# First attention of a fused transformer kernel: the masked queries are made by GpSimd from one unmasked tile, instead of by ScalarE

## The chip, the core and the metric

The kernel runs on one core of one Trainium2 chip. The time is that of the device, in microseconds (us): of several runs the median is taken. Engines are named as the profile names them: PE is TensorE (PEld its loading of weights), DVE is VectorE, ACT is ScalarE, POOL is GpSimd and SP is SyncE, which issues most of the DMAs.

## What is computed

Two layers, each an attention followed by a mixture-of-experts feed-forward. x has 64 sequences of 128 tokens of 128 features, in float32. In short:

```
x = x + attention0(layernorm(x), keys and values from a side input and from a context)
x = x + experts0(layernorm(x))         # 8 experts, the best 2 for each token
x = x + attention1(layernorm(x), keys and values from the context)
x = x + experts1(layernorm(x))         # 8 experts, the best 2 for each token

def attention0(x1, x2, memory):        # 16 heads of 8 features
    q = (x1 @ Wq + bq) split into heads
    k = concatenate(x2 @ Wk + bk, memory) split into heads     # 128 + 120 keys
    v = concatenate(x2 @ Wv + bv, memory) split into heads
    return (softmax(q @ k.T * 8 ** -0.5) @ v) @ Wp + bp
```

The change concerns q of attention0 alone.

## The kernel before

**Heads and slots.** A head has only 8 features, so four heads share a block of 32 partitions. To get the scores of one head out of a matmul over 32 partitions, the queries of the other three are set to zero. Hence every group's queries are stored four times, once for each of NS = 4 slots s, with only the rows of that slot's heads kept: the tile `q4` of 128 partitions x (4 sequences, 4 slots, 128 queries). The mask is a column of `hmask`, a one or a zero for each partition. The rows left empty take the running maximum of the scores later (`shift`, L455 to L464: VectorE adds it into `q4`, L462), so that the second set of matmuls gives scores from which the maximum is already subtracted.

**Groups and iterations.** The 64 sequences are 16 groups g of 4. `attention` (L232) runs one iteration per sequence, and in one iteration several sequences are at different stages. In iteration `it` of the first attention the order of the work is written out by hand (all engines take their instructions in the order in which the program gives them):

- `rounds(0, 1)`: for sequence it, `max_bank` (matmul L394, then the maximum over the keys by VectorE, L414); for sequence it-2, `score_bank` (matmul L430, then the exponential by ScalarE, L438). Each round takes four PSUM banks, two of each kind.
- `out4` (L511), `shift` (transposes L459, then L462), `out5` (L516), statistics of layernorm (`bn_stats`, L109), one call of the router of the experts (`Router.call`, L641).
- `values` (L475, 64 matmuls in four accumulating chains), `out1` (ScalarE's copy L484).
- `prep(it, 0)`, a second call of the router, `rounds(2, 3)`.
- `out3` (L504, L506), `out2` (L491, L495, L497), `prep(it, 1)`.

PSUM is one pool of eight banks (`banks`, tag `bank`); every tile of PSUM is one of them and goes back when its last reader is done.

**Preparing a group's queries.** `prep` (L339) spreads the preparation of the next group over the four iterations of the current one. In the last of them, `prep_x` (L279) transposes the normalized tokens (TensorE, L176) and ScalarE copies them to `xnT` (L177), a tile with a single buffer. In the first iteration of the next group, `prep_q(g, 0)` (L289) runs the matmul with Wq (L292) into one bank and two of ScalarE's activations (L301), and `prep_q(g, 1)`, behind `rounds(2, 3)`, the other two. Each reads the 128x512 bank, adds the bias, applies the mask as its scale and writes one slot of `q4`. So the queries of group g are made in the four iterations ahead of those that read them, except for group 1, where both halves run at the start of iteration 3. Group 0 goes another way (`prep_batch`, L320, four activations of 128x128 for each sequence). `q4` has three buffers. The second attention uses `prep_q` too, and has made an unmasked copy as well (`qfs`, L295).

**GpSimd's queue.** In the first attention GpSimd makes the layernorm (`put_together`, L138 to L146, and the normalization L167), once for the attention itself and once for the router; it adds the output bias to x (L526), computes three products of the router for every second group (L761, L764, L769, between which VectorE reduces, L763, L768, L771) and issues the scatters of the routed tokens (indirect DMA L807, each behind a small copy L806). VectorE takes the router's small steps (`best`, L705, with L718 to L735; `dispatch`, L818, with L836 to L861) in `Router.call`, in between the maxima of the rounds.

**Later stages.** After the first attention, the tiles of the experts (`tile_stage`, L1050), then the second attention with the second set of experts inside it.

Of the kernel before, what the change touches and what calls it, by code (L numbers as in the profile page):

```python
# [8 lines left out]
F32 = mybir.dt.float32  # L9
I32 = mybir.dt.int32  # L10
AF = mybir.ActivationFunctionType
ALU = mybir.AluOpType
# [6 lines left out]
GB = 4  # L19
NG = B // GB  # L20
S = 128
D = 128
# [22 lines left out]
def transformer_kernel(ctx, tc, a, out):  # L45
    nc = tc.nc
# [25 lines left out]
    def load_const(name, shape, src):  # L72
        t = const.tile(shape, F32, name=f"c_{name}", tag=f"c_{name}")
        nc.sync.dma_start(t, src)
        return t

    def load_row(name, n):
        return load_const(name, [128, n], a[name].partition_broadcast(128))

    def attention_weights(p, names=("wq", "wk", "wv", "wo", "bq", "bk", "bv", "bo")):  # L80
        columns = {"bq": NS, "bk": NV, "bqf": 1}
        return {
            n: load_row(p + n, D) if n in ("bv", "bo")
            else load_const(p + n, [D, columns.get(n, D)], a[p + n])
            for n in names
        }

    l0 = attention_weights("a0_", ("wk", "bk"))
# [96 lines left out]
    for s in range(2):  # L185
        k = keep.tile([128, NV, GB, KF + KC], F32, name=f"k2_{s}", tag=f"k2_{s}")
        K2.append(k)
        v = keep.tile([KF, GB, H // 2, 2, 32], F32, name=f"v_{s}", tag=f"v_{s}")
# [43 lines left out]
    def attention(layer, w, norm, first, aside):  # L232
# [5 lines left out]
        with ExitStack() as es:  # L238
            work = es.enter_context(tc.tile_pool(name=f"work{layer}", bufs=2))
# [4 lines left out]
            if first:  # L244
                for s in range(2):
                    v = work.tile([128, GB, H // 2, 2, 32], F32, name="vc", tag="vc")
# [3 lines left out]
            qfs, k4s = {}, {}  # L250
            src, q4s, xnTs, ps_, pavs, pts, ots, normed = {}, {}, {}, {}, {}, {}, {}, {}
# [24 lines left out]
            def mtile():  # L276
                return banks.tile([128, 512], F32, name="bank", tag="bank")
# [11 lines left out]
            def prep_q(g, v):  # L289
                if v == 0:  # L290
                    pqs[g] = mtile()
                    nc.tensor.matmul(pqs[g], lhsT=w["wq"], rhs=xnTs[g], start=True, stop=True)  # L292
                pq = pqs[g]
                if v == 0 and not first:
                    nc.scalar.activation(  # L295
                        qfs[g], pq.rearrange("p (b q) -> p b q", b=GB), AF.Identity,
                        bias=w["bqf"],
                    )
                for i in range(2):
                    s = 2 * v + i  # L300
                    nc.scalar.activation(  # L301
                        q4s[g][:, :, s, :], pq.rearrange("p (b q) -> p b q", b=GB),
                        AF.Identity, bias=w["bq"][:, s : s + 1], scale=hmask[:, s : s + 1],
                    )
# [34 lines left out]
            def prep(it, half):  # L339

                g, j = it // GB + 1, it % GB
                if not first:
                    if g == 1:
                        if (j, half) == (0, 0):
                            prep_k(1)
                            prep_v(1)
                        elif (j, half) == (0, 1):
                            prep_x(1)
                        elif j == 1:
                            prep_q(1, half)  # L350
                            if half:
                                prep_heads(1)
                    elif g < NG:
                        pieces = (
                            (), (lambda: prep_k(g),),
                            (lambda: (prep_heads(g), prep_v(g)), lambda: prep_x(g)),
                            (lambda: prep_q(g, 0), lambda: prep_q(g, 1)),
                        )[j]
                        if half < len(pieces):
                            pieces[half]()  # L360
                    return
# [9 lines left out]
                if (it, half) == (3, 0):  # L371
                    prep_q(1, 0)
                    prep_q(1, 1)
# [923 lines left out]
    aside0 = Aside0()  # L1297
    steps = attention(0, l0, norms[0], True, aside0)
    next(steps)
    l0.update(attention_weights("a0_", ("wq", "bq")))  # L1300
    hmask = load_const("hmask", [128, NS], a["hmask"])
    next(steps)
    l0.update(attention_weights("a0_", ("wv", "bv")))
# [178 lines left out]
def _laid_out(inp):  # L1482

    import numpy as np

    A = {k: np.asarray(v) for k, v in inp.items()}

    def moved(w):
        w = w.reshape(-1, NV, 4, 2 * HD)[:, ::-1]
        return w.transpose(0, 2, 1, 3).reshape(-1, D)  # L1490

    heads = np.arange(D).reshape(4, NV, 2, HD)
    hm, km, sm = (np.zeros((D, n), np.float32) for n in (NS, NV, NV))
    for v in range(NV):
        km[heads[:, 1 - v].ravel(), v] = 1.0
        sm[np.arange(4) * 32 + 16 * v, v] = 1.0
        for i in range(2):
            hm[heads[:, 1 - v, i].ravel(), 2 * v + i] = 1.0

    o = {"x": A["x"]}  # L1500
    o["fsideT"] = A["fside_BxSxS_0"].transpose(2, 0, 1)
    c = A["ctx_1024"]
    o["ctxT"] = c.transpose(2, 0, 1)
    k = moved(c.reshape(B * KC, D)).reshape(B, KC, 1, D)
    o["ctx_k"] = np.where(km.T > 0, k, sm.T).transpose(3, 2, 0, 1)
    v = np.zeros((B, KC, H // 2, 2, 32), np.float32)
    for i in range(2):
        v[:, :, :, i, 16 * i : 16 * i + HD] = c.reshape(B, KC, H // 2, 2, HD)[:, :, :, i]
        v[:, :, :, i, 16 * i + HD] = 1.0
    o["ctx_v"] = v.reshape(B, KC, H * 32).transpose(1, 0, 2)  # L1510
    o["hmask"], o["kmask"], o["smask"] = hm, km, sm
    for p, l, names, tr in (
        ("a0_", "L0_xattn_", ("Wq", "bq", "Wk", "bk", "Wv", "bv", "Wp", "bp"), False),
        ("a1_", "L1_xattn_", ("W_q", "b_q", "W_k", "b_k", "W_v", "b_v", "W_o", "b_o"), True),
    ):
        wq, bq, wk, bk, wv, bv, wo, bo = (A[l + n] for n in names)
        if tr:
            wq, wk, wv, wo = wq.T, wk.T, wv.T, wo.T
        o[p + "wq"], o[p + "wk"] = moved(wq), moved(wk)
        o[p + "bq"] = np.where(hm > 0, moved(bq).T, np.float32(0.0))  # L1520
        if tr:
            o[p + "bqf"] = moved(bq).T
        o[p + "bk"] = np.where(km > 0, moved(bk).T, sm)
        o[p + "wv"], o[p + "bv"] = wv, bv
        o[p + "wo"], o[p + "bo"] = wo, bo
    o["wqkvT"] = A["L0_ffn_wqkv"].T

    w1 = np.zeros((E, D, 2, NF * 128), np.float32)
    w1[..., :F] = A["L0_ffn_w1"].reshape(E, 2, F, D).transpose(0, 3, 1, 2)
    w2 = np.zeros((E, NF * 128, D), np.float32)  # L1530
    w2[:, :F] = A["L0_ffn_w2"].transpose(0, 2, 1)
    w12 = np.concatenate(
        [w1.reshape(E, D, 2, NF, 128).transpose(0, 1, 3, 2, 4).reshape(E, D, NF, 256),
         w2.reshape(E, NF, 128, D).transpose(0, 2, 1, 3)], axis=3,
    )
    o["w12"] = w12.reshape(E, D, NF * 384)
    o["upper"] = np.triu(np.ones((128, 128), np.float32), 1)
    o["ones"] = np.ones((128, 128), np.float32)
    o["steps256"] = np.arange(CAP // TT, dtype=np.float32) * TT

    t = np.zeros((4, 32, 4, 2, 64), np.float32)
    for e in range(E):
        t[:, e, e // 2, e % 2, :] = 1.0
    o["select"] = t.reshape(128, 4, 128)
    o["tiles"] = np.arange(NA, dtype=np.float32).reshape(1, -1)
    o["row_number"] = np.arange(1, 129, dtype=np.float32).reshape(-1, 1)
    o["first_row"] = np.arange(E, dtype=np.float32) * CAP
    o["wgT"] = A["L1_ffn_Wg"].T
    o["bg"] = A["L1_ffn_bg"]
    o["lw1T"] = A["L1_ffn_W1"].transpose(2, 0, 1).reshape(D, E * R)  # L1550
    o["lw2T"] = A["L1_ffn_W2"].transpose(0, 2, 1).reshape(E * R, D)
    return {k: np.ascontiguousarray(v) for k, v in o.items()}
# [18 lines left out]
```

## Time and profile before

| what | value |
|---|---|
| time, median of 3 runs | 1477.64 us (1471.13 to 1481.87) |
| the profiled execution, time | 1476.76 us |
| its span, first to last instruction | 1474.9 us |
| granted TensorE clock, mean | 0.987 |
| instructions | 42033 |
| ACT, all of the four slots (L301), both attentions | 90.1 us busy in 124 instructions |
| POOL, all | 647.0 us busy in 1195 instructions |
| first attention, period of one group | 37.0 to 37.7 us, 41.3 us for the one at 499.7 us |

The times are those of one execution, taken by the hardware profiler. A row of the groups gives a line, an engine and an operation, out<-in by tile names with their shapes, xcount, then busy us and mean ns of one, then how long the engine was idle just before and what ended that. The chain of waits is followed back from the last instruction: at every step to what released it, or to the instruction before it on its engine; it lists start, length and instruction. A timeline lists start, length, engine, line and how many instructions were put together. Matmuls are pipelined and their ends are modelled, so starts are the surer part.

### The profile page before, as it was taken

The page shows a single profiled execution, that of the slowest core. Times are in us where ns is not written, and L with a number is a line of the kernel's source. Part 1 is how long each engine was busy: PE and PEld are TensorE (multiplying, and loading weights), DVE is VectorE, ACT ScalarE, POOL GpSimd, SP SyncE. Part 2 cuts the span into 40 slices and gives each one's busy share as a digit, 9 for nine tenths or more (in the row PEclk, how much of TensorE's full clock was granted, in tenths as well). Part 3 has the DMA queues.
Part 4 walks back from the last instruction along what each step waited for, and adds up shares of the span by engine and source line. Part 5 has one row for each costly group of instructions (what it writes and reads, how often), then busy time and mean ns, then how long its engine had stood idle before and what let it go on. Part 6 is the DMA issues. An engine that isn't in the chain of part 4 may idle for free.

```text
span 1474.9 us, 42033 instructions
## 1 busy us (share of the span) xinstructions
PE 1403.5 (95%) x16620; PEld 1099.4 (75%) x16620; DVE 1111.6 (75%) x3025; ACT 845.2 (57%) x1759; POOL 647.0 (44%) x1195
## 2 busy tenths in 40 slices
PE   7999999999999999999999999898999999999987
PEld 5677777777777777788899998576677677767765
DVE  6777888888888888646574444588988878888863
ACT  3666666666666656643333333466766666766644
POOL 4123346565656554665100131557655666554210
PEclk9999999999999999999999999899999999999999
DMA  8422223333222213247777777301111111110000
GB/s 205 120 77 76 77 77 90 88 92 89 76 64 65 64 44 79 85 141 212 227 215 210 209 215 214 94 28 33 33 30 37 30 40 37 33 30 23 9 16 22
DMA packets 143718, 133.02 MB, mean 90 GB/s; under 512 B 48546, under 2 KB 126114, under 8 KB 141602
## 3 DMA queue, kind: packets, MB, share of 16 engines
q1 hardware_dynamic: 135330, 113.02, 27.9%
q0 software_dynamic: 8192, 17.32, 3.8%
q8 instruction: 132, 2.16, 0.6%
q14 instruction: 64, 0.52, 0.1%
HBM read 97.32 MB, written 32.97 MB: 88 GB/s over the span
## 4 chain that ended last, share of the span: by engine, by line
PE 75%; DVE 17%; POOL 4%; issue 2%; DMA 1%; ACT 1%; SPq 1%; POOLq 0%; DVEq 0%; ACTq 0%
PE bank L430 11%; PE bank L1115 11%; PE bank L394 10%; PE bank L475 9%; DVE nm L414 6%; PE bank L1128 5%; PE bank L1427 4%; PE bank L1450 4%; DVE q L462 2%; PE bank L407 2%; PE bank L214 2%; PE bank L511 2%; PE bank L681 2%; PE bank L202 2%; PE bank L176 2%; PE bank L292 2%
## 5 line engine op out<-in xcount | busy, mean ns | idle before, releaser
L414 DVE TENSOR_REDUCE nm<-bank 128x2 f32<-128x496 f32 (+1 forms) x768 | 463.5, 663 | 82.3 <-PE bank L430 63.2
L438 ACT ACTIVATE p<-bank 120x512 f32<-120x512 f32 (+1 forms) x768 | 402.3, 605 | 130.1 <-PE bank L430 128.4
L430 PE MATMUL bank<-q,k 32*120 32x256 f32 (+1 forms) x3072 | 438.8, 399 | 12.3 <-DVE q L462 5.4
L430 PEld LDWEIGHTS bank<-q,k 32*120 32x120 f32 (+1 forms) x3072 | 294.0, 181 | 51.5 <-DVE nm L414 17.5
L394 PE MATMUL bank<-k,q 32*128 32x248 f32 x2048 | 291.6, 400 | 0.7 <-ACT q L334 0.5
L394 PEld LDWEIGHTS bank<-k,q 32*128 32x128 f32 x2048 | 202.8, 189 | 47.8 <-issue 10.9
L1119 ACT ACTIVATE p<-bank 128x256 f32<-128x256 f32 x213 | 81.0, 384 | 189.3 <-PE bank L1115 189.2
L475 PE MATMUL bank<-p,v 128*32 128x128 f32 (+1 forms) x4096 | 176.2, 276 | 0.3
L1120 DVE TENSOR_TENSOR p<-p,bank 128x256 f32<-128x256 f32 x213 | 86.5, 419 | 89.0 <-ACT p L1119 88.4
L407 PE MATMUL bank<-k,qf 32*128 32x480 f32 x512 | 146.6, 604 | 0.8 <-ACT qf L295 0.8
L807 POOL DMA_INDIRECT xs<-xn,at x128 | 129.6, 1013 | 27.8 <-issue 24.3
L484 ACT COPY ov<-bank 128x256 f32<-128x256 f32 x128 | 48.1, 376 | 142.9 <-PE bank L475 142.9
L475 PEld LDWEIGHTS bank<-p,v 128*32 128x32 f32 (+1 forms) x4096 | 109.3, 110 | 22.7 <-issue 13.8
L1115 PE MATMUL bank<-q 128*128 128x256 f32 x516 | 119.0, 380 | 5.2 <-DMA q<-in_w 3.4
L1367 POOL DMA_INDIRECT yb<-ys,back x112 | 109.0, 973 | 27.7 <-issue 20.9
L167 POOL TENSOR_SCALAR xn<-x,mv,rstd 128x128 f32<-128x128 f32 x252 | 114.3, 465 | 7.1 <-issue 1.0
L462 DVE SCALAR_TENSOR_TENSOR q<-bank,c_smask,q 128x256 f32<-128x256 f32 x256 | 111.1, 476 | 7.2 <-PE bank L459 7.0
L1115 PEld LDWEIGHTS bank<-q 128*128 128x128 f32 x516 | 94.8, 190 | 17.5 <-issue 4.3
L475 PE MATMUL bank<-p,vc 120*32 120x128 f32 x2048 | 103.2, 272 | 0.0
L301 ACT ACTIVATE q<-bank,c_a_bq,c_hmask 128x512 f32<-128x512 f32 x124 | 90.1, 789 | 9.8 <-PE bank L292 9.8
L1157 POOL DMA_INDIRECT kvT<-ys,back x16 | 15.4, 963 | 175.5 <-PE bank L1128 106.4
L138 POOL TENSOR_TENSOR mv<-st 128x4 f32<-128x4 f32 x31 | 6.4, 207 | 196.0 <-DVE st L109 196.0
(227 smaller groups left out, 2469.5 us busy)
## 6 DMA issues: line engine op xcount, KB each, us to landing
q<-in_w SPq DMA_DIRECT2D x43, 576.0 KB, 3.8
vc<-in_w SPq DMA_DIRECT2D x28, 576.0 KB
vc<-in_ctx_v SPq DMA_DIRECT2D x16, 960.0 KB, 7.0
ys<-zero SPq DMA_DIRECT2D x71, 128.0 KB, 1.9
k<-in_ctx_k SPq DMA_DIRECT2D x32, 240.0 KB, 2.8
q<-xs SPq DMA_DIRECT2D x43, 128.0 KB, 2.1
ys<-q SPq DMA_DIRECT2D x43, 128.0 KB, 2.9
x<-in_x SPq DMA_DIRECT2D x16, 256.0 KB, 4.4
```

Source lines behind the costliest of these rows:

```text
L167: nc.gpsimd.tensor_scalar(xn[:, j, :D], xg[g][:, j, :], self.mv[:, b, 0:1], self.rstd[:, b : b + 1], ALU.add, ALU.mult,)
L301: nc.scalar.activation(q4s[g][:, :, s, :], pq.rearrange("p (b q) -> p b q", b=GB), AF.Identity, bias=w["bq"][:, s : s + 1], scale=hmask[:, ...
L394: nc.tensor.matmul(pa[:, u, :], lhsT=q4s[g][r, j, s, :], rhs=k2[g % 2][r, s // 2, j, :], start=True, stop=True,)
L407: lambda: nc.tensor.matmul(pa, lhsT=qfs[g][r, j, :], rhs=k4s[g][r, :, j, :], start=True, stop=True),
L414: nc.vector.tensor_reduce(nm[b % 2].rearrange("q i (a s) -> q a i s", s=16)[:, 2 * ra + v : 2 * ra + v + len(slots) // 2, :, 0], pa.rearra ...
L430: nc.tensor.matmul(pb[:n, v * 256 : (v + 1) * 256], lhsT=k2[g % 2][r, v, j, k0 : k0 + n], rhs=q4s[g][r, j, 2 * v : 2 * v + 2, :].rearrange ...
L438: nc.scalar.activation(ps_[b][:n, c, ra, :], pb[:n], AF.Exp, scale=SCALE)
L462: nc.vector.scalar_tensor_tensor(q, pm, smask[:, v : v + 1], q, ALU.mult, ALU.add)
L475: nc.tensor.matmul(pav[32 * ra : 32 * ra + 32, v * S : (v + 1) * S], lhsT=vs[g % 2][c][:, j, 4 * v + ra, i, :], rhs=p[:n, c, ra, (2 * v + ...
L807: s = nc.gpsimd.indirect_dma_start(xs, bass.IndirectOffsetOnAxis(at[:, j, k : k + 1], 0), xn, None)
L1115: nc.tensor.matmul(ph[:, u, :], lhsT=w[:, c, u * 128 : (u + 1) * 128], rhs=xT, start=True, stop=True)
L1367: nc.gpsimd.indirect_dma_start(y[:, k, b % 2, :], None, ys, bass.IndirectOffsetOnAxis(back[:, b, k : k + 1], 0),)
```

## The change

In the first attention `prep_q(g, 0)` now lets ScalarE write one unmasked tile of queries with its bias (`bqf`, one column) into a buffer of the tag `xnT`, that is, the same single buffer from which the matmul just read. GpSimd then makes the four slots from it: `tensor_scalar`, SBUF to SBUF, with a column of `hmask`, slots 0 and 1 in the first half of `prep_q`, slots 2 and 3 in the second. ScalarE's four activations are not reached any more. The bias `bqf` of the first attention becomes an input of the kernel and is loaded by one more DMA between those of `bq` and `hmask`. Group 0 (`prep_batch`) and the second attention stay.

```
@@ -296,6 +296,17 @@
                         qfs[g], pq.rearrange("p (b q) -> p b q", b=GB), AF.Identity,
                         bias=w["bqf"],
                     )
+                if first:
+
+                    if v == 0:
+                        qfs[g] = work.tile([D, GB * S], F32, name="xnT", tag="xnT", bufs=1)
+                        nc.scalar.activation(qfs[g], pq, AF.Identity, bias=w["bqf"])
+                    for s in range(2 * v, 2 * v + 2):
+                        nc.gpsimd.tensor_scalar(
+                            q4s[g][:, :, s, :], qfs[g].rearrange("p (b q) -> p b q", b=GB),
+                            hmask[:, s : s + 1], None, ALU.mult,
+                        )
+                    return
                 for i in range(2):
                     s = 2 * v + i
                     nc.scalar.activation(
@@ -1297,7 +1308,7 @@
-    l0.update(attention_weights("a0_", ("wq", "bq")))
+    l0.update(attention_weights("a0_", ("wq", "bq", "bqf")))
     hmask = load_const("hmask", [128, NS], a["hmask"])
@@ -1518,8 +1529,7 @@
-        if tr:
-            o[p + "bqf"] = moved(bq).T
+        o[p + "bqf"] = moved(bq).T
```

From L306 on, the lines of the changed kernel are numbered 11 higher (L414 becomes L425, and so on); the new instructions are L303 (ScalarE) and L305 (GpSimd).

## The prediction

> **What bounds the kernel now.** I read the page first (busy time by engine, slices, chain), then the sums by stretch over the first attention, then the chain of waits inside one group of four sequences, then the groups of GpSimd and the timelines around the edited lines.
>
> ```profile
> PE 1403.5 (95%) x16620; PEld 1099.4 (75%) x16620; DVE 1111.6 (75%) x3025; ACT 845.2 (57%) x1759; POOL 647.0 (44%) x1195
> L301 ACT ACTIVATE q<-bank,c_a_bq,c_hmask 128x512 f32<-128x512 f32 x124 | 90.1, 789 | 9.8 <-PE bank L292 9.8
> ```
>
> TensorE is busy almost throughout, ScalarE and GpSimd are not. The 124 instructions of L301 are 60 of the first attention (15 groups of 4; group 0 is made by prep_batch) and 64 of the second; only the 60 go. Removing 60 of them frees ScalarE, but ScalarE is no bound, so the value lies in who waits for it.
>
> ```profile
> 88.20:125.20 37.00, 36.60 (x573) 27.84 (x572) 28.19 (x63) 23.82 (x48) 9.68 (x28) 1.00 0.30 77
> 312.20:349.90 37.70, 37.19 (x577) 28.34 (x576) 32.74 (x89) 24.03 (x49) 20.61 (x49) 1.00 0.35 91
> ```
>
> Columns: length, then busy PE, PEld, DVE, ACT, POOL. Each stretch is one group period, from one prep_q to the next. The later one holds 4.55 us more VectorE and 10.9 us more GpSimd work (the router), and is only 0.7 us longer, of which 0.56 is a TensorE matmul of the router (L831). So TensorE sets the period, and VectorE has a little room.
>
> Inside one group the chain of waits shows where TensorE itself stops:
>
> ```profile
> 303.14 0.40 PE bank L394
> ...
> 305.04 0.26 PE bank L504
> ...
> 306.23 0.40 PE bank L394
> ...
> 308.64 0.42 PE bank L511 x2
> ...
> 311.18 1.06 PE bank L292 x2
> 312.23 0.40 PE bank L394
> ...
> 313.32 0.67 DVE nm L414
> ...
> 314.03 0.47 PE bank L430
> ...
> 315.15 0.26 PE bank L504
> ...
> 315.62 0.40 PE bank L394
> ...
> 318.58 0.42 PE bank L511 x2
> ```
>
> rounds(2, 3) run from the first L394 to L504, rounds(0, 1) of the next iteration from L394 to L511. An ordinary rounds(2, 3) takes 305.04-303.14 = 1.90. The one behind prep_q takes 315.15-312.23 = 2.92, with a stop for VectorE's maximum (L414) in it. Reason: the pool has eight PSUM banks. prep_q's bank is held by its second pair of L301, which stands behind rounds(2, 3) on ScalarE; rounds(2, 3) want eight, so the eighth must come from a maximum of the same rounds. The following rounds(0, 1) take 2.96, against 2.41 (306.23 to 308.64) and 2.83 (324.94 to 327.77, the iteration after).
>
> **The change, part by part.**
>
> Removed: four activations a group (0.784 each), in two pairs. Added on ScalarE: one of 128x512 with a bias alone; the same form is L295's row, 0.690. It ends about 312.27+0.69 = 312.96, and prep_q's bank is free then, ahead of 313.3 where TensorE stopped. The changed program's TensorE stream agrees: behind L292 the eighth bank's first matmul waits for ScalarE where it waited for VectorE. So rounds(2, 3) go from 2.92 to 1.90: 1.02. rounds(0, 1) lose the second pair ahead of their exponentials, 2.96 to between 2.83 and 2.41; VectorE's four maxima (2.4 us) follow directly on those of rounds(2, 3), so I take 2.83: 0.13. Together 1.15 a group; groups 2 to 15: 14 x 1.15 = **-16.1** (at most 1.57 x 14 = -22.0; at least 0, if another wait steps in).
>
> Added on GpSimd: four TENSOR_SCALAR 128x512 a group, 60 in all. No such row exists.
>
> ```profile
> L167 POOL TENSOR_SCALAR xn<-x,mv,rstd 128x128 f32<-128x128 f32 x252 | 114.3, 465 | 7.1 <-issue 1.0
> L526 POOL TENSOR_TENSOR x<-x,c_a_bo 128x512 f32<-128x512 f32 x30 | 38.7, 1289 | 2.4
> L806 POOL COPY spacer<-rs 1x1 f32<-1x1 f32 x96 | 17.0, 177 | 14.4 <-DVE rs L495 13.8
> L823 POOL COPY chosen<-one 128x64 f32<-128x64 f32 x16 | 3.9, 241 | 0.0
> ```
>
> Upper end: four times L167, four of which take 1.75 back to back: 1.75. Lower end: a copy, 177 + 511 x (241-177)/63 = 0.70. The nearest row is L167, same operation; its fixed part is about 0.16 (distance of the tiny L138 and L139), so (0.437-0.16)/128 x 512 + 0.16 = 1.27, which is also L526's 1.289. I take **1.29**, and 5.16 a group. That is 14% of a period in which GpSimd is busy at most 22.8 of 37.2, so GpSimd is not the bound. The q tiles have four iterations (some 37 us) until rounds read them. So the latency itself costs nothing in groups 2 to 15; what covers it is prep running one group ahead.
>
> **What the added work delays.** In GpSimd's order (of the changed program) the four come after the router's normalization (L167) and a pair of scatters (L807), so around 312 they would start when the last scatter ends, 317.62+0.97 = 318.6, and end at 323.8. Two things stand in the way.
>
> (a) VectorE. A VectorE instruction that reads and writes only SBUF can be stopped for the whole of a GpSimd one:
>
> ```profile
> 1241.38 1.30 POOL L526 TENSOR_TENSOR x<-x,c_a_bo 128x512 f32<-128x512 f32 x1
> 1241.48 1.47 DVE L313 TENSOR_SCALAR k<-k,c_hmask 128x480 f32<-128x480 f32 x1
> ```
>
> L313's median is 0.466. Likewise L719, with two SBUF inputs, took 0.76 instead of 0.22 beside L1379. L414, L462 and L516, which read PSUM, show the same duration with and without GpSimd work beside them. In every router group VectorE runs a cluster of such small instructions (L718 to L734, or the two L858 and L861) just there:
>
> ```profile
> 320.88 0.21 DVE L718 TENSOR_TENSOR eq<-r,m 128x64 f32<-128x64 f32 x1
> ```
>
> With the 1.15 saved it begins at 319.7, inside 318.6 to 323.8. I take it that one instruction of the cluster gets through per GpSimd instruction, as L719 beside L1379 shows; so L718 ends at 320.0, L719 at 321.35, L723 at 322.7, L732 at 324.1, and the maxima behind them start at 324.8, when TensorE had them ready at 322.4: 2.4 late. Behind that the timeline shows idle time of VectorE before it holds TensorE: 1.08 (before L221) and 0.27. I take 2.4-1.35 = 1.0 on TensorE. This meets the 8 groups whose prep_q lies from 237 to 500 (before, no scatters push the four so late; in the last group two more pairs push them past the cluster): 8 x 1.0 = **+8.0**.
>
> (b) GpSimd's own queue. Behind the four stand the norm of the next group, scatters, L526 and, every other group, the router's product L761; VectorE's L763 waits for it in order. In the group at 275 the four would run 281.5 to 286.7 where L138 started at 283.85, and no idle time lies between that and L761. L761 then ends 293.7+2.8 = 296.5, and L763, which ran at 294.9, is 1.6 to 1.9 late; VectorE's idle time after it is 0.60+0.64. 0.7 a case, 4 cases (275, 350, 425, 500): **+2.8**. The scatters and norms are later too, by about 3 us, but the transposes that need the norm come some 11 us after it.
>
> (c) Start. For group 1 prep_q and its use lie one iteration apart, GpSimd idle. Its slots are done at 43.5+5.16 = 48.7 and not 45.5. The first two suffice for rounds(0, 1), at 46.1 against 47.5 before. But the new tile lies in the single xnT buffer, so prep_x's copy (L177, 47.60 before), with ScalarE's queue behind it, waits for 48.7: first exponential 49.3 against 48.62. **+0.6**, from -1 (short instructions) to +2.5.
>
> (d) One more DMA of 512 B on SP's queue, 0.43 of issue and 0.05 between, in front of hmask and all later loads. The mask was issued at 4.14, and ScalarE first uses it at 10.13, after TensorE; the context keys, issued until 5.6 with 2.8 to landing, at 10.6. About 2 us of cover: 0 (without it 0.5).
>
> Sum: -16.1+8.0+2.8+0.6 = **-4.7**. The profiled execution took 1476.76 (span 1474.9), 0.9 below the median of 1477.64; 1476.76-4.7 = **1472**.
>
> A rule that speaks against the change: the Trainium skill, GPSIMD Engine Reference, section 4.1 (Engine selection), would put elementwise multiplication on VectorE. The same page, section 3.1, gives 769 ns as a best case for 512 elements with a tight loop, where L167 here scales to 1.27 us. By 0.77 the four would take 3.1 us, (a) and (b) would nearly vanish, and the estimate from that page would be about -16.
>
> **Rivals.**
>
> 1. Short instructions, faster (0.70 each). The four end at 321.4; the cluster is delayed by about 0.7, which the 0.77 of VectorE's idle time before the maxima takes up, and L138 by 0.35. Sum -16.1-0.5: **1460**. For it: a copy's slope. Against it: L167, the same operation.
>
> 2. Long instructions, slower: VectorE shut out. At 1.75 the four run to 325.6 and four VectorE instructions wait in turn; maxima at 326.5, 4.1 late, 2.7 on TensorE: 8 x 2.7 = 22. L763 2.2 late on TensorE x 4 = 9; start 2.5. Sum +17: **1494**. It outweighs the gain from about 1.4 us an instruction (costs 11.4 at 1.29 and 33 at 1.75). For it: rows of 128 lie apart in the output. Against it: L526 handles 4x128 in 1.29.
>
> 3. The bank comes free, but the wait passes to VectorE's maxima, which follow one another without a gap in the neighbouring iteration: nothing saved, costs stay: 1476.8+11.4 = **1488**. Against it: ordinary rounds(2, 3) of 1.90 with the same VectorE work.
>
> **Chances.** Forecast 0.53, rival 1 0.25, rival 2 0.13, rival 3 0.09. 1% of the time, about what a measurement of this kernel can tell from no change, is 14.8: faster means below 1462.9, slower above 1492.4. Faster: 0.7 of rival 1 and the forecast's edge, 0.20. Slower: over half of rival 2, the edge of rival 3 and unseen waits, 0.12. Same 0.68. Range: forecast alone 1464 to 1480; for 8 in 10, 1457 (rival 1 with some of the 1.57) to 1488 (rival 3, up to rival 2's lower part).
>
> **What would show it.** Right: the rounds(2, 3) behind L292 at 1.9, no stop on L414 there; periods 1.1 shorter up to 237 us; the multiplication at 1.2 to 1.4 us; L719, L723, L732 or L858 lengthened to about 1.3 after 237 us, and periods there only some 0.2 shorter; L763 waiting for L761. Wrong: a period that stays 37.0 before 237 us (rival 3); instructions of 0.7 (rival 1) or 1.75 (rival 2); TensorE waiting for GpSimd's q tile at all; the second attention changed.

## The result and the profile after

The changed kernel takes **1487.82 us** (median of 8 runs, 1485.82 to 1492.5) against 1478.33 for the kernel before on the same chip (8 runs): a ratio of 1.0072, interval 1.0055 to 1.009. It is slower by about 10 us, where 5 us less were forecast. The profiled execution has a span of 1487.0 us and a granted clock of 0.983.

Two rows of the profile, busy time by engine and the group of the new multiplication:

```profile
PE 1401.1 (94%) x16620; PEld 1101.1 (74%) x16620; DVE 1119.1 (75%) x3025; ACT 817.8 (55%) x1714; POOL 737.5 (50%) x1255
L305 POOL TENSOR_SCALAR q<-xnT,c_hmask 128x512 f32<-128x512 f32 x60 | 93.1, 1569 | 20.3 <-ACT xnT L303 19.9
```

ScalarE has lost 27 us, GpSimd has gained 90: 60 multiplications of 1.57 us, not 1.29. In the rows from here on L394 is L405, L414 is L425, L504 is L515, L761 is L772 and L763 is L774.

The sums by stretch: an early group, then two neighbouring groups with the router, each from one prep_q to the next (columns as before: length, then busy PE, PEld, DVE, ACT, POOL; clock, DMA share, GB/s):

```profile
91.32:127.14 35.82, 35.73 (x572) 27.58 (x568) 27.89 (x65) 21.94 (x45) 15.80 (x31) 1.00 0.31 80
274.44:315.04 40.60, 36.82 (x573) 28.02 (x569) 31.68 (x80) 22.68 (x46) 28.70 (x50) 0.96 0.32 85
315.04:352.78 37.74, 36.63 (x576) 28.32 (x572) 34.55 (x86) 22.09 (x46) 26.78 (x53) 1.00 0.34 91
```

The early group is 1.15 shorter than before (36.97), as forecast. The second one is 3.4 *longer* than before (37.19), with 3.8 us in which TensorE is not busy and a clock below 1. The third is as long as before (37.71).

The chain of waits in the early group, from prep_q's matmul to the end of rounds(2, 3):

```profile
91.39 1.06 PE bank L292 x2
92.45 0.40 PE bank L405
...
94.35 0.26 PE bank L515
```

94.35-92.45 = 1.90 where it was 2.92, and no maximum (L425) stands in it any more: the bank does come free, and the gain is there. The loss is elsewhere. In the group at 274 us the chain runs over GpSimd for 23 us; the four multiplications together are called the train below:

```profile
274.57 0.20 POOL mv L138
...
282.05 6.23 POOL q L305 x4
288.27 0.17 POOL mv L138
...
295.64 1.26 POOL x L537
296.90 1.04 POOL pp L772
297.96 0.69 DVE r L774
298.65 0.59 DVE nm L425
299.24 0.04 issue
299.28 0.33 PE bank L515
```

The same place in VectorE's and in TensorE's timeline (start, length, what; in brackets the idle time before it and what ended it):

```profile
297.96 0.69 DVE L774 TENSOR_REDUCE r<-pp 128x64 f32<-128x512 f32 x1 [3.57 <-POOL pp L772]
```

```profile
299.28 0.33 PE L515 MATMUL bank<-ident,o 128*128 128x128 f32 x1 [3.66 <-DVE nm L425]
299.45 0.38 PE L502 MATMUL bank<-ident,ov 128*128 128x128 f32 x2
299.86 1.84 PE L202 MATMUL bank<-kvT,c_a_wk 128*128 128x512 f32 x2
```

VectorE waits 3.57 us for the router's product, with the maxima queued behind the waiting L774; TensorE, whose L515 is released by the first of these maxima, stops for 3.66. Afterwards its matmuls take almost twice their time (L202's pair 1.84, against 1.08 to 1.13 in the groups whose clock is whole), and the sums by stretch show why in their clock, the column after the six busy times:

```profile
296.30:299.70 3.40, 0.42 (x3) 0.31 (x3) 1.74 (x3) 0.47 (x1) 3.07 (x6) 1.00 0.59 136
299.70:303.10 3.40, 3.37 (x20) 1.63 (x21) 1.73 (x5) 1.63 (x3) 3.22 (x5) 0.57 0.39 121
```

And at the start ScalarE stands still for the four multiplications, since prep_x's copy (L177) wants the single xnT buffer:

```profile
49.78 0.59 ACT L177 COPY xnT<-bank 128x512 f32<-128x512 f32 x1 [3.94 <-POOL q L305]
```

TensorE stops in its turn, for ScalarE's copy:

```profile
50.42 0.48 PE L441 MATMUL bank<-q,k 32*128 32x256 f32 x1 [2.57 <-ACT xnT L177]
```

A smaller wait of the same kind as the one at 298 us stands in the group at 199 us, 22 us behind its start, where TensorE stops for 0.90:

```profile
220.50 0.69 DVE L774 TENSOR_REDUCE r<-pp 128x64 f32<-128x512 f32 x1 [0.81 <-POOL pp L772]
```

### The profile page after: what moved, and what is told of

It reads as the page before. It is cut to its first block, busy times and chain, and to the rows that moved or that the text cites. A ratio compares the mean times of both kernels' runs of the same rounds, so it can differ in the third digit from the quotient of the medians.

```text
span 1487.0 us, 42013 instructions
## 1 busy us (share of the span) xinstructions
PE 1401.1 (94%) x16620; PEld 1101.1 (74%) x16620; DVE 1119.1 (75%) x3025; ACT 817.8 (55%) x1714; POOL 737.5 (50%) x1255
## 4 chain that ended last, share of the span: by engine, by line
PE 61%; DVE 21%; POOL 10%; DMA 3%; issue 2%; SPq 2%; ACT 1%; POOLq 0%; DVEq 0%; ACTq 0%
PE bank L1126 10%; DVE nm L425 8%; PE bank L441 7%; PE bank L486 7%; PE bank L405 7%; PE bank L1139 5%; PE bank L1438 4%; PE bank L1461 4%; DVE q L473 3%; PE bank L418 2%; POOL q L305 2%; PE bank L202 2%; POOL xs L818 2%; POOL xn L167 2%; PE bank L522 1%
## 5 line engine op out<-in xcount | busy, mean ns | idle before, releaser
L425 DVE TENSOR_REDUCE nm<-bank 128x2 f32<-128x496 f32 (+1 forms) x768 | 460.2, 661 | 72.9 <-PE bank L441 59.9
L441 PE MATMUL bank<-q,k 32*120 32x256 f32 (+1 forms) x3072 | 432.9, 400 | 12.9 <-DVE q L473 5.4
L441 PEld LDWEIGHTS bank<-q,k 32*120 32x120 f32 (+1 forms) x3072 | 295.9, 182 | 40.6 <-DVE q L473 10.6
L405 PE MATMUL bank<-k,q 32*128 32x248 f32 x2048 | 288.3, 400 | 1.2 <-ACT q L345 0.5
L405 PEld LDWEIGHTS bank<-k,q 32*128 32x128 f32 x2048 | 206.6, 191 | 55.0 <-issue 18.3
L1126 PE MATMUL bank<-q 128*128 128x256 f32 x516 | 122.4, 388 | 6.4 <-DMA q<-in_w 4.5
L167 POOL TENSOR_SCALAR xn<-x,mv,rstd 128x128 f32<-128x128 f32 x252 | 114.4, 467 | 7.4 <-issue 1.2
L305 POOL TENSOR_SCALAR q<-xnT,c_hmask 128x512 f32<-128x512 f32 x60 | 93.1, 1569 | 20.3 <-ACT xnT L303 19.9
L155 POOL TENSOR_SCALAR rstd<-mv 128x4 f32<-128x4 f32 x32 | 6.4, 199 | 189.0 <-DVE mv L113 102.6
```

What stands on the lines that cost most here:

```text
L167: nc.gpsimd.tensor_scalar(xn[:, j, :D], xg[g][:, j, :], self.mv[:, b, 0:1], self.rstd[:, b : b + 1], ALU.add, ALU.mult,)
L305: nc.gpsimd.tensor_scalar(q4s[g][:, :, s, :], qfs[g].rearrange("p (b q) -> p b q", b=GB), hmask[:, s : s + 1], None, ALU.mult,)
L405: nc.tensor.matmul(pa[:, u, :], lhsT=q4s[g][r, j, s, :], rhs=k2[g % 2][r, s // 2, j, :], start=True, stop=True,)
L425: nc.vector.tensor_reduce(nm[b % 2].rearrange("q i (a s) -> q a i s", s=16)[:, 2 * ra + v : 2 * ra + v + len(slots) // 2, :, 0], pa.rearra ...
L441: nc.tensor.matmul(pb[:n, v * 256 : (v + 1) * 256], lhsT=k2[g % 2][r, v, j, k0 : k0 + n], rhs=q4s[g][r, j, 2 * v : 2 * v + 2, :].rearrange ...
L1126: nc.tensor.matmul(ph[:, u, :], lhsT=w[:, c, u * 128 : (u + 1) * 128], rhs=xT, start=True, stop=True)
```

## The experiments

Theory 1: the loss is a queue that is late. The train of four stands in GpSimd's order ahead of the router's product, VectorE waits for that in order, TensorE stops and its clock then halves; at the start the shared buffer does the same through ScalarE. The rival is the prediction's own larger term, contention: VectorE shut out of SBUF while GpSimd multiplies.

All ratios are to the kernel before, on the same chip (95% interval). "us" is the ratio's distance from 1 times 1477.

| kernel | ratio | us |
|---|---|---|
| the change | 1.0072 (1.0055 to 1.009) | +10.6 |
| slot 3 instead of xnT | 1.0037 (1.0023 to 1.0051) | +5.5 |
| norm later | 0.998 (0.9968 to 0.9992) | -3.0 |
| both | 0.9916 (0.9893 to 0.994) | -12.4 |
| multiplications later | 0.9889 (0.9869 to 0.9909) | -16.4 |
| cost alone | 1.0079 (1.0063 to 1.0096) | +11.7 |
| multiplications later, on VectorE | 0.9938 (0.9921 to 0.9955) | -9.2 |
| gain alone, on ScalarE | 0.9882 (0.9859 to 0.9904) | -17.4 |
| three multiplications on GpSimd | 1.0007 (0.9991 to 1.0022) | +1.0 |
| split multiplications | 1.0064 (1.0041 to 1.0087) | +9.5 |

Group periods from their profiles, worked out as distances between the starts of prep_q's matmuls (L292 before):

| stretch | before | change | slot 3 | norm later | both | mult. later | cost alone | gain alone | three |
|---|---|---|---|---|---|---|---|---|---|
| first to second | 10.04 | 14.57 | 8.89 | 14.97 | 8.89 | 12.99 | 10.03 | 10.38 | 10.66 |
| next | 35.53 | 35.20 | 34.39 | 34.81 | 34.39 | 34.39 | 35.52 | 34.39 | 34.39 |
| group at 87 us | 36.97 | 35.82 | 35.83 | 35.82 | 35.82 | 35.83 | 36.96 | 35.82 | 35.82 |
| 199 | 37.19 | 36.95 | 37.18 | 36.06 | 36.06 | 36.06 | 37.18 | 36.05 | 36.05 |
| 236 | 37.71 | 37.75 | 37.73 | 37.77 | 37.34 | 36.75 | 38.63 | 36.56 | 38.02 |
| 274 | 37.19 | 40.59 | 40.83 | 36.70 | 36.81 | 36.06 | 39.77 | 36.05 | 39.07 |
| 311 | 37.71 | 37.75 | 37.72 | 37.77 | 37.34 | 36.74 | 37.74 | 36.56 | 38.03 |
| 349 | 37.19 | 40.59 | 40.82 | 36.69 | 36.81 | 36.06 | 41.76 | 36.05 | 38.17 |
| last (499) | 41.18 | 41.52 | 42.70 | 40.64 | 38.70 | 40.15 | 40.69 | 40.02 | 40.21 |

The stretches are named by the us at which they start before the change. Those at 199, 274, 349 and 424 us, in which VectorE waits for the router's product, are called even, those at 236, 311, 386 and 461 us odd. The groups at 424 and 386, 461 us repeat those at 274 and 311. The stretch behind them, from the last prep_q of the first attention to the first of the second, differs between executions by some 3 us either way (399.9 before, 402.8 the change, 396.7 to 401.3 the others; the split version, on another chip, is left out), in no order that follows the edits; so small differences are read from the periods, not from the spans.

### Slot 3 instead of the xnT buffer

```diff
+            def masked(g, slots, engine=None):
+                for s in slots:
+                    (engine or nc.gpsimd).tensor_scalar(
+                        q4s[g][:, :, s, :], q4s[g][:, :, 3, :], hmask[:, s : s + 1], None, ALU.mult
+                    )
...
-                        qfs[g] = work.tile([D, GB * S], F32, name="xnT", tag="xnT", bufs=1)
-                        nc.scalar.activation(qfs[g], pq, AF.Identity, bias=w["bqf"])
-                    for s in range(2 * v, 2 * v + 2):
-                        nc.gpsimd.tensor_scalar(
-                            q4s[g][:, :, s, :], qfs[g].rearrange("p (b q) -> p b q", b=GB),
-                            hmask[:, s : s + 1], None, ALU.mult,
+                        nc.scalar.activation(
+                            q4s[g][:, :, 3, :], pq.rearrange("p (b q) -> p b q", b=GB),
+                            AF.Identity, bias=w["bqf"],
                         )
+                    masked(g, range(2 * v, 2 * v + 2))
```

> ScalarE writes the unmasked queries into slot 3 of the q tile instead of the single xnT buffer; GpSimd makes slots 0 to 2 from it and slot 3 last, in place. Nothing else is moved. Theory 1 (the loss of 10 us is GpSimd's queue being late, so that TensorE stops for over 3 us and its clock then halves; and the start, where ScalarE's L177 waits 3.94 us for the tile): the stretch from the first to the second prep_q goes from 14.57 us to about 9.5 (before: 10.04), all the rest stays; time 1483 (5 less than the changed kernel). The periods of 40.59 us at 275, 349 and 424 us stay. Rival (shared SBUF contention is the main loss, VectorE shut out by long GpSimd instructions): the same at the start if the wait on the tile is its cause; if the start is slow because of GpSimd's traffic, no change at all, 1488.

Measured: 1481.58 us, first stretch 8.89, the one behind it 34.39; the periods at 274, 349 and 424 us stay at 40.8. As theory 1 said: the wait for the tile is the whole loss at the start (5.7 us and 0.8 of half clock behind it), and it isn't the main loss.

### Norm later

```diff
-                if first and it % GB == 2:
-                    norm_of(it // GB + 2)
...
                     aside.end(it, work, mtile)
+                    if it % GB == 2:
+                        norm_of(it // GB + 2)
```

> The changed kernel, with the norm of the next group (in GpSimd's queue L138 to L167 and the addition of the bias) issued at the end of the iteration and not at its start, so that the router's product pp (L772 of the changed kernel) stands 3.0 us earlier in GpSimd's queue. The four multiplications, their length and their place beside VectorE's cluster stay. Theory 1 (late queue): VectorE's wait for pp (3.57 us at 298) falls to about 0.5, TensorE no longer stops for over 3 us, its clock stays up, and the three periods of 40.59 become 36.5 to 37.2; time 1475 to 1477. Rival (contention with long GpSimd instructions): those periods stay at 40.6, time 1488.

Measured: 1474.09, 13.6 less than the change by the ratios. Multiplications, their length and place are the same; only L167 and the addition L537 have moved behind the product. The wait that carried the loss, in this kernel:

```profile
291.77 0.69 DVE L774 TENSOR_REDUCE r<-pp 128x64 f32<-128x512 f32 x1 [0.55 <-POOL pp L772]
```

3.57 has become 0.55, the period 40.59 has become 36.70; the group at 199 us goes from 36.95 to 36.06 as well. The odd groups (236, 311) stay at 37.77. So the main loss is the order of GpSimd's queue, and contention is at most what the odd groups show: 37.77-36.56 = 1.2 each.

### Both

The two diffs together.

> The two edits together: slot 3 instead of the xnT buffer, and the norm at the end of the iteration. Theory 1: both losses go and add up, start 5 less and three periods 4 less each: 1470 to 1472, 0.4 to 0.6% under the kernel before. Rival (contention is the main loss): 1483 to 1488.

Measured: 1463.17. Both losses go, and 4 us more than their sum: 2 in the last group (38.70), 0.4 in each odd group; why was not followed up. This is theory 1's version of the change, and it beats the kernel before by 0.84%.

### Multiplications later

Against the version with slot 3:

```diff
-                    masked(g, range(2 * v, 2 * v + 2))
+                    if g == 1:
+                        masked(g, range(2 * v, 2 * v + 2))
...
                 elif (j, half) == (2, 1):
                     prep_k(g)
+                    if it > GB:
+                        masked(g, range(NS))
```

(masked() is that of the first experiment.)

> Slot 3 instead of the xnT buffer, and from group 2 on the four multiplications are issued two iterations later, behind prep_k, where GpSimd has already made the product pp (L772) and its successor (L775). The norm stays where it was. Theory 1: no late pp, no multiplication beside VectorE's cluster of the odd groups (there 1.2 us a group in the changed kernel), so periods of 36.0 in nearly all groups; 1464 to 1468. What could spoil it is the third product (L780): GpSimd idles 4.0 us ahead of it and the four take 6.2, so it may be 2 us late in four groups, with up to 4 us each if TensorE stops again: then 1475 to 1480. Rival (contention): it moves to whatever VectorE does beside the four in the new place, and only the start gets better: 1480 to 1484.

Measured: 1459.8. The even groups take 36.06 and the odd 36.75, within 0.2 of the gain alone: the same 60 multiplications, still 1.57 each, cost nearly nothing in this place (1 us by the ratios, whose intervals overlap). GpSimd is as busy in the group at 267 us (29.00) as it was in the change's (28.70), in 36.06 us instead of 40.60:

```profile
266.57:302.63 36.06, 35.94 (x572) 27.57 (x569) 31.28 (x80) 22.45 (x46) 29.00 (x50) 1.00 0.36 95
302.63:339.37 36.74, 36.54 (x577) 28.14 (x573) 32.88 (x86) 22.02 (x46) 26.77 (x53) 1.00 0.35 94
```

The first stretch came to 12.99 here: TensorE waited 3.40 us for a DMA of the context keys, and this execution had reached that point 1.8 us before that of the first experiment, while SyncE had issued this DMA 4.2 us later (40.40 against 36.20). Why it was issued later was not followed up.

### Cost alone

```diff
                         AF.Identity, bias=w["bq"][:, s : s + 1], scale=hmask[:, s : s + 1],
                     )
+                if first:
+                    for s in range(2 * v, 2 * v + 2):
+                        nc.gpsimd.tensor_scalar(
+                            q4s[g][:, :, s, :], q4s[g][:, :, s, :], hmask[:, s : s + 1], None, ALU.mult
+                        )
```

> The kernel before, with ScalarE's four masked activations left as they are, and behind each pair two GpSimd multiplications of the same slots by the same mask, in place (a second multiplication by 0 or 1 changes nothing). So it has all of the added GpSimd work and none of the gain, and the xnT buffer isn't used. Theory 1: the train of four takes its 6.2 us in the same place of GpSimd's queue, so the three periods of 37.19 at 275, 349 and 424 us become 41 to 42, the odd groups from 237 us on (37.71) about 1.2 longer, the start between 0 and 1 longer, the periods up to 237 us unchanged at 36.97 to 37.71: +17 to +20 us, 1494 to 1497. Rival (contention): the added time is spread over all eight router groups, 1 to 2.5 us each.

Measured: 1489.03, +11.7 and not +17 to +20. The even periods are 39.77, 41.76 and 39.76; the clock halves behind one of the three stops. VectorE's wait in the group at 275 us:

```profile
299.04 0.69 DVE L768 TENSOR_REDUCE r<-pp 128x64 f32<-128x512 f32 x1 [2.50 <-POOL pp L766]
```

2.50 here, 3.57 in the change, with the same train in the same place of the queue. The difference, 1.07, is the gain: with it TensorE and VectorE come 1.15 earlier to a product that comes no earlier. So gain and cost don't add up. In a group whose period GpSimd's queue sets, the gain is worth nothing. The odd groups, for which 1.2 more had been expected, stay at 37.74 (37.71 before; the one at 236 us alone took 38.63). There VectorE's cluster of small instructions falls otherwise on the multiplications: in the group at 311 us its seven take 2.71 us from first start to last end (1.72 before, 3.67 in the change), rounds(2, 3) beside it take 0.46 more than before, and the rounds(0, 1) behind them 0.37 less.

### Multiplications later, on VectorE

Against "Multiplications later":

```diff
-                        masked(g, range(NS))
+                        masked(g, range(NS), nc.vector)
```

> As the version with the multiplications two iterations later, but from group 2 on VectorE makes them and not GpSimd (for group 1 they are where they were, on VectorE's queue too only from group 2 on). Four of about 0.5 us (L313, 128x480, has 0.466) are 2.0 us of VectorE in one piece, behind the router's and the maxima's work of that half iteration. If VectorE has that room there (busy 28 to 33 of a period of 36), 1459 to 1462, as with GpSimd. If VectorE's queue is what TensorE waits for next, up to 2.0 us in each of 14 groups comes back: up to 1488. I take 0.7 of it a group: 1470.

Measured: 1468.57, near the 1470 taken. Four take 1.97 us on VectorE:

```profile
291.51 1.97 DVE L291 TENSOR_SCALAR q<-q,c_hmask 128x512 f32<-128x512 f32 x4
```

The periods are 36.05 in the early groups (35.82 with the gain alone), 36.45 in the even and 37.52 in the odd. The instruction is three times shorter on VectorE, and yet dearer there: in the odd group at 236 us TensorE waits 0.85 us for VectorE behind it, at a matmul of the router, where it waits 0.11 with the gain alone:

```profile
259.65 0.41 PE L849 MATMUL bank<-m,c_upper 128*128 128x64 f32 x2 [0.85 <-DVE s L766]
```

So VectorE's queue is nearer to TensorE's path than GpSimd's in this place.

### Gain alone, on ScalarE

Against the change, with the buffer replaced by slot 3 as in the first experiment:

```diff
+            def masked(g, *slots):
+                for s in slots:
+                    nc.scalar.activation(
+                        q4s[g][:, :, s, :], q4s[g][:, :, 3, :], AF.Identity, scale=hmask[:, s : s + 1]
+                    )
...
+                    if g == 1:
+                        masked(g, *((0, 1), (2, 3))[v])
+                    else:
+                        masked(g, v)
...
+                elif j == 1 and it > GB:
+                    masked(g, 2 + half)
```

> The gain alone, with no multiplication on GpSimd: ScalarE writes the unmasked queries from PSUM into slot 3 (which frees the bank) and then makes the slots itself from that copy: slot 0 at once, slot 1 behind rounds(2, 3), slots 2 and 3 an iteration later; for group 1 all in one iteration. ScalarE has one instruction of 0.7 to 0.8 a group more than in the kernel before. Theory 1: rounds(2, 3) behind prep_q at 1.9 in all groups, periods of 35.8 to 36.6, no other change: 14 x 1.15 = 16.1 less than the kernel before, 1459 to 1463. Rival (the wait passes to VectorE's maxima or ScalarE's exponentials): 1470 to 1480.

Measured: 1460.7. The periods are 1.15 shorter than before in every group from the second stretch on, odd and even (36.56 and 36.05), and so the prediction's first term is confirmed: 1.15 a group to its second digit. The first stretch is not shorter (10.38); TensorE waits 1.77 us there for the context keys.

### Three multiplications on GpSimd

```diff
-                    for s in range(2 * v, 2 * v + 2):
+                    for s in range(2 * v, min(2 * v + 2, 3)):
...
+                    if v == 1:
+                        nc.scalar.activation(
+                            q4s[g][:, :, 3, :], qfs[g].rearrange("p (b q) -> p b q", b=GB),
+                            AF.Identity, scale=hmask[:, 3:4],
+                        )
```

> The changed kernel with three multiplications on GpSimd instead of four; slot 3 is made by ScalarE from the copy in SBUF, behind rounds(2, 3). So pp (L772) is made 1.57 us earlier. This tells a plain wait from one that also halves TensorE's clock. Theory 1 with the clock: in the groups at 275, 349 and 424 us TensorE's stop falls from some 3.6 to 2.0 us, which is too short to halve its granted clock, so the period falls by more than 1.57: from 40.59 to about 38.1. Without the clock effect: 40.59-1.57 = 39.0. By contention: 40.2. At the start ScalarE's wait for the tile falls by 1.57, TensorE's stop from 4 us to some 2.5: the first stretch 14.57 becomes 11 to 13. Time 1476 to 1479.

Measured: 1477.26, first stretch 10.66, the three periods 39.07, 38.17 and 39.07. VectorE's wait is 2.03 to 2.05 and TensorE's stop 2.12 to 2.14 in all three; what differs is the clock of the 4 us behind the stop:

```profile
291.20:295.20 4.00, 4.00 (x30) 2.51 (x34) 1.86 (x5) 1.75 (x3) 3.35 (x6) 0.57 0.43 106
...
368.30:372.30 4.00, 4.00 (x37) 2.52 (x38) 3.37 (x8) 2.97 (x6) 3.65 (x6) 1.00 0.49 122
...
444.40:448.40 4.00, 4.00 (x28) 2.74 (x32) 2.17 (x6) 2.04 (x5) 3.64 (x6) 0.59 0.41 112
```

So the stop costs its length (38.17-36.05 = 2.12) and a halved clock 0.90 more. The expectation held for one case of three: its rule, that only a stop of over 3 us halves the clock, fell (see the last section). The odd groups took 38.0, 0.3 more than with four. The place is another rounds(2, 3), 20 us into the group, 2.79 instead of 2.10; why it is longer was not followed up.

### Split multiplications

"Both", with this edit:

```diff
-                    nc.gpsimd.tensor_scalar(
-                        q4s[g][:, :, s, :], q4s[g][:, :, 3, :], hmask[:, s : s + 1], None, ALU.mult
-                    )
+                    for b in range(GB):
+                        nc.gpsimd.tensor_scalar(
+                            q4s[g][:, b, s, :], q4s[g][:, b, 3, :], hmask[:, s : s + 1], None, ALU.mult
+                        )
```

> As the version with slot 3 and the late norm, with each GpSimd multiplication of 128x512 cut into four of 128x128, one for each sequence (16 a group). Two questions. The price: by the two rows L167 (0.437 for 128 elements) and L305 (1.566 for 512) a multiplication costs 0.06 + 2.94 ns an element, so the train should take 16 x 0.437 = 7.0 us instead of 6.3; with the fixed part of 0.16 of the prediction it would have been less a row and 4 x 1.27 in the whole. The contention: if VectorE's small instructions wait for the end of a whole GpSimd instruction (as the prediction took it), waits of up to 1.57 become waits of at most 0.44, and the odd groups' rounds(2, 3) beside the cluster fall from 3.10 to about 2.3, the period from 37.34 to about 36.7. If the two engines share the access in smaller pieces, the cluster is slowed as much as before: periods of 37.3 to 37.6, time 1463 to 1467.

Measured: 1553.9, on a chip on which the kernel before took 1543.66 (the stages behind the first attention are slower there); by the ratio 1.0064, 1.5% worse than unsplit (two chips, each against the kernel before on its own). The price was wrong again:

```profile
L292 POOL TENSOR_SCALAR q<-q,c_hmask 128x128 f32<-128x128 f32 x240 | 139.8, 598 | 11.1 <-ACT q L309 10.8
```

One starts every 0.579 us, where L167, the same operation on as many elements, has 0.437. With 1.54 between starts at 512 elements this form costs 0.26 + 2.50 ns an element. The train takes 9.3 us, the product is late again, TensorE stops for 3.66 three times, and the even periods are 42. On contention: the odd rounds(2, 3) beside the cluster take 2.70, between the 3.10 of no change and the 2.3 of the whole-instruction rule; the cluster itself lasts 2.8 us instead of 3.2 (1.7 with the gain alone). That doesn't decide it.

## Why the prediction was wrong

**The gain, -16.1: right.** 1.15 a group, mechanism and size; measured alone at -17.4 (-20.8 to -14.2), and visible in the change up to 199 us.

**The price, 1.29: too low.** 1.57. L167's fixed part isn't the one of this form, and a bound of 1.75 was named; rival 2 gave 1.4 as the point from which the loss outweighs the gain. The train is 6.23 us and not 5.16. Rival 1 (0.70 each) is out by the same row. By the Trainium skill, GPSIMD Engine Reference, section 3.1, a best case of 0.77 stood beside it; this trace shows twice that.

**(a) Contention, +8.0: about 4.8, and not as described.** The four odd groups lost 37.75-36.56 = 1.19 each, and keep this loss when only the norm is moved; with the multiplications in another place it falls to 36.75-36.56 = 0.19. In the even ones TensorE's stop behind the product and the halved clock account for the whole loss. The cluster in the change, beside multiplications that start at 322.54, 324.11, 325.64 and 327.18:

```profile
323.87 0.33 DVE L729 TENSOR_TENSOR eq<-r,m 128x64 f32<-128x64 f32 x1
324.24 0.64 DVE L730 TENSOR_TENSOR eq<-eq,order 128x64 f32<-128x64 f32 x1
324.91 0.22 DVE L732 TENSOR_REDUCE at<-eq 128x8 f32<-128x64 f32 x1
325.17 0.58 DVE L734 TENSOR_TENSOR one<-order,at 128x64 f32<-128x64 f32 x1
325.78 0.82 DVE L743 TENSOR_SCALAR cap<-one 128x64 f32<-128x64 f32 x1
326.63 0.66 DVE L745 TENSOR_TENSOR rest<-r,cap 128x64 f32<-128x64 f32 x1
327.32 0.22 DVE L746 TENSOR_REDUCE m<-rest 128x8 f32<-128x64 f32 x1
```

With the gain alone each takes 0.19 to 0.23:

```profile
309.07 0.22 DVE L739 TENSOR_TENSOR eq<-eq,order 128x64 f32<-128x64 f32 x1
309.84 0.19 DVE L752 TENSOR_SCALAR cap<-one 128x64 f32<-128x64 f32 x1
```

Five are held up, by 0.1 to 0.65 and not to 1.3 each, and more than one passes beside one multiplication: L730 ends at 324.88, 0.8 before the end of the multiplication that it runs beside, and L743 0.6 before that of its own.

**(b) GpSimd's queue, +2.8: about 16. This is the step that failed.** "L763, which ran at 294.9, is 1.6 to 1.9 late; VectorE's idle time after it is 0.60+0.64. 0.7 a case" (its two numbers give 0.4 to 0.7). Measured: three cases of 40.59-36.05 = 4.54, 41.52-40.02 = 1.5 in the last group (with a half-clock interval in both executions), and 0.90 in the group at 199 us, which the prediction did not count: there TensorE's stop is behind the late product too, and it goes with the norm moved. Four things were missing, all in the rows above: 1.07 from the price; 1.07 because the change's own gain brings VectorE earlier to the wait, while the queue that it waits for stays; the idle time of VectorE absorbed nothing, since TensorE's stop (3.66) is as long as the wait (3.57); and 0.9 from the halved clock. With the 1.6 of the prediction these give 1.6+1.07+1.07+0.9 = 4.6, against 4.54.

**(c) The start, +0.6: about 5.** Named with its mechanism and bounded by 2.5; ScalarE waited 3.94 with the exponentials behind L177, the first of them came at 50.27 and not 49.3, TensorE stopped for 2.57, and 6.8 us at half clock followed, which the prediction had no term for. Removed, it gave 5.7 and 0.8; against the kernel before the loss is 4.53 in the first stretch and 0.8 behind it.

**(d) The DMA, 0:** the first stretches don't contradict it; it wasn't tried by itself.

Sum of the measured terms: -16.1+4.8+16.0+5.3 = +10.0, against +10.6 by the ratio. Of the rivals, the second came nearest (longer instructions, from 1.4 on a loss), but for the wrong reason: it put two thirds of its cost on VectorE shut out of SBUF, where most of it is GpSimd's order. Rival 3 (no gain) is out by the early periods, though it named 1488. The change of 0.7% is within the 1% that had the largest chance, and the time lies at the upper edge of the range of 1457 to 1488; the sign was wrong. That the range reaches so far is luck: its upper end was set by rival 3 and by the lower part of rival 2, and neither is what happened.

## What to carry to other kernels

Work moved to an idle engine is priced by what stands behind it in that engine's queue, not by the engine's busy share: against the gain alone, the same 60 instructions cost 28 us in one place of GpSimd's order (5 of them through the buffer) and about 1 us, within the intervals, in another. A gain and a cost on different engines don't add up: where the cost's queue sets the period, the gain only brings the others earlier to the wait. And a new tile in a buffer that exists only once should be followed to the next writer of it, and to all that stands behind that writer.

## What the runs showed of the hardware

**The clock.** In all eleven traces of this case the granted clock changes only at multiples of 3.41 us from one another. For each such interval of the first attention from 60 to 550 us in which the clock was whole, TensorE's idle time was added up (from the modelled ends of matmuls). Up to 1.50 us idle the clock never halved (1.09 to 1.50: 14 intervals); from 1.66 to 3.36 it halved in the next interval every time (18 of 18); between them 1.59 halved and 1.62 didn't. So a stop of 2.14 us halves it or not by where it falls: 2.17 of it in one interval at 288 us, halved; 1.11 and 1.04 in two at 365 us, not. The Trainium skill, TensorE: Matmul & The Clock Gate, part 1, has the free-running window of 3413 ns, which agrees; its rule of no idle gaps above some 3.4 us (section "HAM oscillation") is too kind here, since somewhat under half an interval is enough by these rows.

**The shared access to SBUF.** The Trainium skill, SBUF — State Buffer, section "Who interferes with whom", says that an instruction of VectorE with two inputs in SBUF contends with one of GpSimd that reads SBUF, and that a reduction doesn't; its section "SBUF: two separate sides" says that whichever starts first holds the shared access for its whole instruction. The rows above agree with the first two (L729, L730, L734 and L745, with two inputs, are longer, L732 and L746 keep their 0.22) and not with the third: L730 ends at 324.88, before the next multiplication starts at 325.64.
